# A graph network on one core: the edge matrix counted by 64 destinations and two source halves, and one-hots made eight tiles at a time

## The chip, the cores and the metric

The kernel runs on one core of one Trainium2 chip. The metric is the device time of one execution in microseconds (us). The kernel before takes 3625.48 us, the median of 10 runs (3618.81 to 3635.07).

The core's engines run side by side, each with its own instruction stream: TensorE (PE, matmuls into PSUM banks, with its weight loads shown as PEld), VectorE (DVE), ScalarE (ACT), GpSimd (POOL) and SyncE (SP). On GpSimd stand the indirect DMAs that gather rows from device memory by an index; SyncE issues most of the other DMAs.

## The reference

6250 nodes of 128 features, 100,000 edges sorted by destination, 8 edge types. Two networks follow each other, each added to its input and normalised:

```python
def _rgcn_conv(x, src, dst, etype, bases_l, comp_l, root_l, bias_l):
    weight = jnp.einsum('rb,bio->rio', comp_l, bases_l)
    h = jnp.einsum('ni,rio->nro', x, weight)
    msg = h[src, etype]
    seg = dst * R + etype
    cnt = jax.ops.segment_sum(jnp.ones((msg.shape[0],), dtype=x.dtype), seg, num_segments=N * R)
    norm = 1.0 / jnp.maximum(cnt[seg], 1.0)
    agg = jax.ops.segment_sum(msg * norm[:, None], dst, num_segments=N)
    return agg + x @ root_l + bias_l
...
# first network: 3 such layers, batch norm and relu behind the first two
# second network:
    h = x @ W_in + b_in
    deg = jax.ops.segment_sum(jnp.ones(row.shape[0], dtype=h.dtype), row, num_segments=N)
    deg_inv_sqrt = jnp.where(deg > 0, jax.lax.rsqrt(jnp.maximum(deg, 1.0)) * jnp.where(deg > 0, 1.0, 0.0), 0.0)
    edge_weight = deg_inv_sqrt[row] * deg_inv_sqrt[col]
    acc = h
    cur = h
    for _ in range(NUM_LAYERS):            # 3
        msgs = cur[col] * edge_weight[:, None]
        cur = jax.ops.segment_sum(msgs, row, num_segments=N)
        acc = acc + cur
    final = acc / (NUM_LAYERS + 1)
    return final @ W_out + b_out
```

In the second network `row` is the source and `col` the destination of an edge.

## The kernel before

Everything that runs is in one function, `sorted_path`; a second path behind a flag (`general_path`) is for inputs of another kind and does not run here. Nodes lie in 49 blocks of 128 (`NBLK`), edges in 782 tiles of 128 (`NTS`).

**The gathers and sums.** Each of the three layers of the first network goes over the edge tiles. For tile t, `one_sum` (line 1470) issues one indirect DMA on POOL that fetches 128 rows of 128 floats (line 1472) into `gt`, lets VectorE make a weighted one-hot `o` (line 1476: the edge's column compared with a row of numbers, times the edge's weight `norm`; 56 columns wide in the first kind of sum, 48 in the second), and lets PE multiply the two into a PSUM bank (line 1478). `gt` comes from a pool of 32 buffers (`gp`), `o` from one of 16 (`op`), the PSUM banks `ps` from one of 2, each holding 8 sums. Tiles 92 to 191 (`first_sums`, 100 gathers a layer) fetch rows of the layer's input x and VectorE adds the sum to `z` (line 1496). Tiles 192 to 781 (`window_sums`, 590 gathers a layer) fetch messages from `h_d`; two tiles share a sum, and VectorE adds it to `agg` (line 1526) at a column that a register holds. The messages of a layer, 49 blocks, are made during `first_sums` by `messages` (line 816: two matmuls of 512 columns on PE, copies on ScalarE, a DMA to `h_d`). Tiles 0 to 91 have no gathers: `dense_sums` (line 1180) does them with a small count matrix, in each layer after 400 tiles of the second kind; it loads that matrix in 7 pieces `packed1`.

**The side work.** `side_work` (line 1443) makes three things for later, in small steps that `take_turns` mixes with the tiles of all three layers, `N_SIDE` steps spread over `TURNS` tiles:
- `hot_counts` (line 1011) makes the count matrix for the first 92 tiles, written to `c1_d`.
- `degrees` (line 1257) counts edges per source: per four tiles VectorE makes `lo_hot` (line 1272, 4 x 128) and `blk_hot` (line 1275, 4 x 49), and PE multiplies them (line 1284).
- `counts` (line 1296) makes the whole edge matrix of the second network as small integers, seven counts in the bit fields of one int32 word (`NF` = 7, a field is 7 source blocks of 128, `S` = 896 columns). It works in 245 steps (`NST`) of 4 tiles. A step belongs to one block of 128 destinations. Per step VectorE makes `dst_hot` (line 1405, 4 x 128), and per tile a `row` (line 1409: `iota_c` compared with the edge's source column, times the value of its field, 896 wide); PE multiplies them in two halves of 448 columns (line 1420), two tiles behind (`LEAD` = 2); at a step's last tile VectorE adds the two PSUM banks to the running block `had` (line 1428, two instructions, times a flag that clears it at a new block), and SyncE writes the block to `a_d` (line 1437) under a condition that holds only where the block is done, at a place read from a register.

`rp` (4 buffers) holds `row`, `ac` (4) holds `had`, `cp` (2) holds `dst_hot`, `lo_hot` and `blk_hot`, `ps_w` (5 banks) every `pw`.

**The last stage.** Behind the layers the three rounds of the second network multiply the whole edge matrix with the nodes: per round and slice of sources, 7 loads of 448 KB from `a_d` (`packed`, line 1721), three masks on VectorE (lines 1725 and 1728) and 49 matmuls per load that read single bytes of the words as 8-bit floats (line 1736).

**What sets the order.** The kernel is written for the Tile framework: its scheduler fixes each engine's order when the kernel is built, and a tile's buffer is handed on when its last reader is done. Nothing is reordered at run time: an engine waits at each instruction for its semaphores. POOL's stream between the layers' starts is gathers alone.

## Time and profile before

| | |
|---|---|
| median of 10 runs | 3625.48 us (3618.81 to 3635.07) |
| the profiled execution | 3627.07 us, of which the span from first to last instruction 3625.3 us |
| PE (matmul) | 2835.5 us busy, 78% |
| PEld (weight load) | 2048.8 us, 57% |
| DVE | 2496.6 us, 69% |
| ACT | 320.5 us, 9% |
| POOL | 2169.1 us, 60% |
| mean granted PE clock | 0.734 of full speed |
| HBM | read 231.16 MB, written 211.53 MB |

The groups of instructions that the change touches (count, total busy time, mean of one):

| line | engine | what | count | busy us | mean ns |
|---|---|---|---|---|---|
| 1472 | POOL | gathers from `h_d` | 1770 | 1861.2 | 1052 |
| 1476 | DVE | `o`, 48 wide | 1770 | 476.9 | 324 |
| 1476 | DVE | `o`, 56 wide | 300 | 92.3 | 328 |
| 1478 | PE | sums of `gt` and `o` | 4140 | 968.9 | 348 |
| 1405 | DVE | `dst_hot` | 245 | 166.4 | 679 |
| 1409 | DVE | `row`, 896 wide | 980 | 491.5 | 513 |
| 1420 | PE | `row` x `dst_hot`, 448 columns | 1960 | 735.2 | 506 |
| 1428 | DVE | `had`, 448 columns | 490 | 311.1 | 673 |
| 1736 | PE | last stage, 193 columns | 7203 | 614.7 | 248 |

The share of an engine is an average over stages that have different limits: the layers run to about 2930 us of the span, and the last stage from there. "Busy" leaves out the issuing of DMAs and the handling of registers and semaphores. In lines of a timeline the columns are: start in us, duration in us, engine, line, operation, output and inputs, and in brackets the idle time of the engine before it with what ended it. In the table by stages (windows) each row gives from:to in us, the length, the busy time and number of instructions of each engine, the granted clock, the share of time that the DMA engines were busy and what they moved.

### The profile page before, as it was taken

What the parts mean: (1) busy time and instruction counts of PE and PEld (TensorE: products, weight loads), DVE (VectorE), ACT (ScalarE), POOL (GpSimd) and SP (SyncE); (2) the same over time, 40 slices, a digit from 0 to 9 for tenths busy, and PEclk for the clock granted to TensorE, in tenths of its full rate; (3) what the DMA queues carried; (4) which work ended last, traced back from release to release, by engine and by line L of the source; (5) the groups of instructions that cost most, each with busy time, mean ns of one, the idle gap of its engine ahead of it and who ended that gap; (6) DMA issues with size and microseconds to landing.
All of it is one profiled execution on the core that took longest, in us unless ns stands there. A gap on an engine that the chain in (4) does not pass through costs nothing.

```text
span 3625.3 us, 52477 instructions
## 1 busy us (share of the span) xinstructions
PE 2835.5 (78%) x16544; PEld 2048.8 (57%) x16544; DVE 2496.6 (69%) x7582; ACT 320.5 (9%) x586; POOL 2169.1 (60%) x2083
## 2 busy tenths in 40 slices
PE   5967555668769877877777797887777669999998
PEld 3545344445444455555545454554444469999997
DVE  8557797794782887777548559787764667566555
ACT  2500000001015100000100430000001020000000
POOL 5577897777747777777777477777777720000000
PEclk9955555578769855555776897556567779999998
DMA  5612201124138222222332762222223233333331
GB/s 175 239 52 66 71 21 48 50 56 101 51 87 307 81 61 60 61 66 65 96 76 66 244 221 76 70 71 72 76 80 87 66 102 109 114 112 114 108 117 32
DMA packets 255407, 347.15 MB, mean 96 GB/s; under 512 B 85926, under 2 KB 184078, under 8 KB 255124
## 3 DMA queue, kind: packets, MB, share of 16 engines
q1 hardware_dynamic: 180440, 204.30, 17.6%
q0 software_dynamic: 66240, 135.79, 14.5%
q10 hardware_dynamic: 8444, 3.61, 0.4%
q8 instruction: 138, 2.26, 0.3%
q14 instruction: 145, 1.19, 0.1%
HBM read 231.16 MB, written 211.53 MB: 122 GB/s over the span
## 4 chain that ended last, share of the span: by engine, by line
PE 45%; DMA 24%; DVE 18%; issue 9%; POOL 3%; DVEq 1%; ACT 0%; POOLq 0%; ACTq 0%; SPq 0%
DMA gt<-h_d,gidx 22%; PE pw L1736 16%; PE ps L1478 8%; PE pw L820 6%; PE pw L1420 6%; PE pw L1223 4%; DVE o L1476 3%; POOL gt L1472 3%; DVE row L1409 3%; DVE had L1428 2%; DVE lo_hot L1272 2%; DVE agg L1526 1%; PE pw L1250 1%; PE pw L833 1%; DVE dst_hot L1405 1%
## 5 line engine op out<-in xcount | busy, mean ns | idle before, releaser
L1472 POOL DMA_INDIRECT gt<-h_d,gidx x1770 | 1861.2, 1052 | 539.4 <-issue 198.7
L1478 PEld LDWEIGHTS ps<-o,gt 128*128 128x128 f32 x4140 | 907.0, 269 | 932.2 <-DVE o L1476 280.1
L1478 PE MATMUL ps<-o,gt 128*128 128x48 f32 (+1 forms) x4140 | 968.9, 348 | 545.4 <-DMA gt<-h_d,gidx 341.5
L1420 PE MATMUL pw<-row,dst_hot 128*128 128x448 bf16 x1960 | 735.2, 506 | 52.0 <-DVE row L1409 48.3
L1736 PE MATMUL pw<-three,u 128*128 128x193 bf16 x7203 | 614.7, 248 | 12.2 <-DVE three L1657 9.8
L1736 PEld LDWEIGHTS <-u 128*128 128x128 fp8e3 x7203 | 603.7, 98 | 18.0 <-issue 9.8
L1476 DVE TENSOR_SCALAR o<-iota_f,lo,norm 128x48 f32<-128x48 f32 x1770 | 476.9, 324 | 40.4 <-PE ps L1478 40.0
L1409 DVE TENSOR_SCALAR row<-iota_c,e_tab,e_tab 128x896 bf16<-128x896 int16 x980 | 491.5, 513 | 18.1 <-PE pw L1420 18.0
L1428 DVE SCALAR_TENSOR_TENSOR had<-had,keep,pw 128x448 int32<-128x448 int32 x490 | 311.1, 673 | 206.1 <-PE pw L1420 206.0
L1420 PEld LDWEIGHTS <-dst_hot 128*128 128x128 bf16 x1960 | 287.4, 162 | 218.3 <-issue 179.3
L820 PE MATMUL pw<-w,xT 128*128 128x512 f32 x588 | 289.3, 623 | 0.5 <-DVE xc L1584 0.3
L1472 POOL DMA_INDIRECT gt<-x_d,xidx x200 | 190.1, 951 | 134.3 <-DMA xc<-x_d 36.8
L1728 DVE TENSOR_SCALAR u<-packed 128x896 int32<-128x896 int32 x147 | 91.5, 622 | 187.4 <-PE pw L1736 185.1
L1476 DVE TENSOR_SCALAR o<-iota_f,hcol,norm 128x56 f32<-128x56 f32 x300 | 92.3, 328 | 156.8 <-PE ps L1478 156.3
L1526 DVE TENSOR_TENSOR agg<-agg,ps 128x48 f32 x885 | 171.9, 194 | 24.1 <-PE ps L1478 21.8
L821 ACT COPY hs<-pw 128x512 f32<-128x512 f32 x294 | 170.3, 586 | 172.2 <-PE pw L820 154.5
L1223 PE MATMUL pw<-x,u 128*128 128x385 bf16 x735 | 177.0, 380 | 0.0
L1725 DVE TENSOR_SCALAR u<-packed 128x896 int32<-128x896 int32 x294 | 174.5, 617 | 0.0
L1405 DVE TENSOR_TENSOR dst_hot<-iota_f,e_tab 128x512 bf16<-128x512 f32 x245 | 166.4, 679 | 0.0
L1272 DVE TENSOR_TENSOR lo_hot<-iota_f,e_tab 128x512 bf16<-128x512 f32 x196 | 133.1, 679 | 40.0 <-PE pd L1284 39.6
L820 PEld LDWEIGHTS pw<-w,xT 128*128 128x128 f32 x588 | 106.0, 197 | 87.9 <-issue 76.1
L1223 PEld LDWEIGHTS <-u 128*128 128x128 fp8e3 x882 | 100.8, 117 | 75.1 <-issue 37.5
(371 smaller groups left out, 1690.8 us busy)
## 6 DMA issues: line engine op xcount, KB each, us to landing
a_d<-had SPq DMA_DIRECT2D x245, 448.0 KB
h_d<-hs SPq DMA_DIRECT2D x147, 512.0 KB
packed<-a_d SPq DMA_DIRECT2D x147, 448.0 KB
gt<-h_d,gidx POOLq DMA_INDIRECT x1770, 2.6
c_d<-had SPq DMA_DIRECT2D x62, 196.0 KB
packed<-c_d SPq DMA_DIRECT2D x21, 448.0 KB
x_d<-xc SPq DMA_DIRECT2D x24, 256.0 KB
xc<-in_x_dram SPq DMA_DIRECT2D x19, 256.0 KB
```

Source lines behind the costliest of these rows:

```text
L820: nc.tensor.matmul(ph, xT[:, b * P : (b + 1) * P], w[:, c : c + 512], start=True, stop=True)
L1223: nc.tensor.matmul(sums[d][:, :C3D], us[d % 2][:, i, :, d // 2], x3[:, i, :], start=(c == 0 and i == 0), stop=(c * CH + i == NBLK - 1))
L1272: nc.vector.tensor_tensor(hot[:, :n, :], iota_f[:, None, :].to_broadcast([P, n, P]), src_lo[:, t0 : t0 + n, None].to_broadcast([P, n, P]), ...
L1405: nc.vector.tensor_tensor(hots[s], iota_f[:, None, :].to_broadcast([P, TS, P]), rel_s[:, s, :, None].to_broadcast([P, TS, P]), op=OP.is_equal)
L1409: nc.vector.tensor_scalar(rows[i], iota_c, e_src[:, s, j : j + 1], e_val[:, s, j : j + 1], op0=OP.is_equal, op1=OP.mult)
L1420: nc.tensor.matmul(p[:, :w], hots[s][:, j, :], row[:, c : c + w], start=(j == 0), stop=(j == TS - 1))
L1428: nc.vector.scalar_tensor_tensor(now[:, c : c + w], had[:, c : c + w], keep[:, s : s + 1], p[:, :w], op0=OP.mult, op1=OP.add)
L1472: nc.gpsimd.indirect_dma_start(out=gt, out_offset=None, in_=table, in_offset=bass.IndirectOffsetOnAxis(ap=at[:, t : t + 1], axis=0))
L1476: nc.vector.tensor_scalar(o[:, :width], iota_f[:, :width], column[:, t : t + 1], norm[:, t : t + 1], op0=OP.is_equal, op1=OP.mult)
L1478: nc.tensor.matmul(pa, gt, o[:, :width], start=first_, stop=last)
L1526: nc.vector.tensor_add(to, to, pa)
L1736: nc.tensor.matmul(out_of(f), bytes_[WHERE[f][0]][:, d, :, WHERE[f][1]], cur[:, order[c0 + d], :], start=(c0 + d == 0 and f == f0), stop=( ...
```

## The change

The edge matrix is counted by blocks of 64 destinations (`BD`, 98 blocks) and not 128. The 128 rows of a step's product are the 64 destinations, each once for the lower and once for the upper half of the 896 source columns: an edge whose source column is 448 or more gets its row number moved by 16384 (`FAR`), and `iota_h`, against which `dst_hot` compares, counts 0, 16384, 1, 16385 and so on. So `row` is 448 wide (`SH`), a tile takes one matmul and one PSUM bank, a step one add, and a block in `a_d` is one piece of 1792 bytes per partition. There are 294 steps in place of 245. `row` runs six tiles ahead of its matmul (`LEAD`), the add and the write come three steps of the loop behind the last matmul (`leave`, `LAG`).

The one-hots `o` of eight tiles are made by two instructions, one that compares and one that multiplies by the weights (`hot_columns`), half a batch ahead (`columns_of`).

Pools: `gp` 24 buffers in place of 32, `op` 3 tiles of eight one-hots in place of 16 of one, `rp` 10 (of half the width) in place of 4, `dst_hot` 3 in place of 2, `packed1` 2 in place of 1, loaded two pieces ahead. The last stage reads the same words from the new order of `a_d`, in 896 pieces of 512 bytes per load instead of 128 of 3584. The few instructions in `counts` that turned a block's number into its place (`fld`, `pos`) are gone.

```diff
--- before
+++ after
@@ -601,9 +601,15 @@
     TS = 4
+    BD = P // 2
+    NBD = NP // BD
+    SH = S // 2
+    FAR = 1 << 14
     NG4 = Q * J // TS
-    NST = NG4 + NBLK
-    LEAD = 2
+    NST = NG4 + NBD
+    LEAD = 6
+    LAG = 3
+    OB = 8
     CH = 7
...
@@ -680,8 +686,8 @@
     hp = tc.alloc_tile_pool(name="hp", bufs=3)
-    gp = tc.alloc_tile_pool(name="gp", bufs=32)
-    op = tc.alloc_tile_pool(name="op", bufs=16)
+    gp = tc.alloc_tile_pool(name="gp", bufs=24)
+    op = tc.alloc_tile_pool(name="op", bufs=3)
     xT = first.tile([P, NP], F32, name="xT")
...
@@ -981,15 +987,18 @@
     kp = tc.alloc_tile_pool(name="kp", bufs=1)
-    rp = tc.alloc_tile_pool(name="rp", bufs=4)
+    rp = tc.alloc_tile_pool(name="rp", bufs=10)
     ac = tc.alloc_tile_pool(name="ac", bufs=4)
     dn = tc.alloc_tile_pool(name="dn", bufs=1)
     cp = tc.alloc_tile_pool(name="cp", bufs=2)
 
 
-    a_d = dram.tile([NSL, P, NBLK, P], I32, name="a_d")
-    iota_c = kp.tile([P, S], mybir.dt.int16, name="iota_c")
-    nc.gpsimd.iota(iota_c, pattern=[[1, S]], base=0, channel_multiplier=0)
+    a_d = dram.tile([NBD, P, SH], I32, name="a_d")
+    iota_c = kp.tile([P, SH], mybir.dt.int16, name="iota_c")
+    nc.gpsimd.iota(iota_c, pattern=[[1, SH]], base=0, channel_multiplier=0)
+    iota_h = kp.tile([P, P], F32, name="iota_h")
+    nc.gpsimd.iota(iota_h.rearrange("p (d q) -> p d q", q=2), pattern=[[1, BD], [FAR, 2]], base=0,
+                   channel_multiplier=0, allow_small_or_imprecise_dtypes=True)
     iota_s = kp.tile([P, NST], F32, name="iota_s")
...
@@ -1184,16 +1194,16 @@
         def load(c):
-            packed = dn.tile([P, SUB, CH, R], I32, name="packed1")
+            packed = dn.tile([P, SUB, CH, R], I32, name="packed1", bufs=2)
             nc.sync.dma_start(packed, c1_d[:, :, c * CH * R : (c + 1) * CH * R]
                               .rearrange("p s (d r) -> p s d r", r=R))
             return packed, [(k, n, rows_of(x_d[l], c * CH + k, n, nc.sync)) for k, n in ((0, 4), (4, CH - 4))]
 
-        ready = load(0)
+        ready = [load(0), load(1)]
         for _ in range(3):
             yield
         for c in range(NBLK // CH):
-            packed, parts = ready
+            packed, parts = ready.pop(0)
             nc.scalar.copy(x3[:, :4, :D], parts[0][2])
...
@@ -1215,8 +1225,8 @@
                                         x3[:, k : k + n, D : 2 * D], op=OP.subtract)
-            if c + 1 < NBLK // CH:
-                ready = load(c + 1)
+            if c + 2 < NBLK // CH:
+                ready.append(load(c + 2))
             yield
...
@@ -1390,54 +1388,55 @@
         nc.vector.scalar_tensor_tensor(e_src, e_fld, -float(S), e_src, op0=OP.mult, op1=OP.add)
+        upper = over
+        nc.vector.tensor_scalar(upper, e_src, float(SH), None, op0=OP.is_ge)
+        nc.vector.scalar_tensor_tensor(e_src, upper, -float(SH), e_src, op0=OP.mult, op1=OP.add)
+        nc.vector.scalar_tensor_tensor(rel_s, upper, float(FAR), rel_s, op0=OP.mult, op1=OP.add)
         yield
 
-        pieces = [(c, S // 2) for c in range(0, S, S // 2)]
-        had = ac.tile([P, S], I32, name="had")
+        had = ac.tile([P, SH], I32, name="had")
         nc.vector.memset(had, 0)
-        at = {}
+        at, runs = {}, [had]
         rows, hots, sums = {}, {}, {}
-        for i in range(NST * TS + LEAD):
-            s, j = divmod(i, TS)
-            if s < NST:
-                if j == 0:
-                    hots[s] = cp.tile([P, TS, P], BF16, name="dst_hot")
-                    nc.vector.tensor_tensor(hots[s], iota_f[:, None, :].to_broadcast([P, TS, P]),
-                                            rel_s[:, s, :, None].to_broadcast([P, TS, P]),
-                                            op=OP.is_equal)
-                rows[i] = rp.tile([P, S], BF16, name="row")
-                nc.vector.tensor_scalar(rows[i], iota_c, e_src[:, s, j : j + 1], e_val[:, s, j : j + 1],
-                                        op0=OP.is_equal, op1=OP.mult)
-            if i < LEAD:
-                yield
-                continue
-            s, j = divmod(i - LEAD, TS)
-            open_sums[0] = j < TS - 1
-            if j == 0:
-                sums[s] = [ps_w.tile([P, 512], F32, name="pw") for _ in pieces]
-            pa, row = sums[s], rows.pop(i - LEAD)
-            for (c, w), p in zip(pieces, pa):
-                nc.tensor.matmul(p[:, :w], hots[s][:, j, :], row[:, c : c + w], start=(j == 0),
-                                 stop=(j == TS - 1))
-            if j < TS - 1:
-                yield
-                continue
-            del sums[s], hots[s]
-            now = ac.tile([P, S], I32, name="had")
-            for (c, w), p in zip(pieces, pa):
-                nc.vector.scalar_tensor_tensor(now[:, c : c + w], had[:, c : c + w], keep[:, s : s + 1],
-                                               p[:, :w], op0=OP.mult, op1=OP.add)
+
+        def leave(s):
+            now = ac.tile([P, SH], I32, name="had")
+            nc.vector.scalar_tensor_tensor(now, runs.pop(), keep[:, s : s + 1], sums.pop(s)[:, :SH],
+                                           op0=OP.mult, op1=OP.add)
             if s % REGS == 0:
-                for k, top_ in ((0, NBLK - 1), (1, 1)):
+                for k, top_ in ((0, NBD - 1), (1, 1)):
                     _, v = nc.values_load_multi_w_load_instructions(
                         step_i[0:1, k, s : min(s + REGS, NST)], engines=[ET.SP], min_val=0, max_val=top_,
                         skip_runtime_bounds_check_because=IN_RANGE)
                     for i, x_ in enumerate(v):
                         at[k, s + i] = x_
-            nc.sync.dma_start(
-                a_d[:, :, bass.ds(at[0, s], 1), :].rearrange("s p d c -> p s (d c)"),
-                now.rearrange("p (s c) -> p s c", c=P), cond=(at[1, s] == 1))
-            had = now
+            nc.sync.dma_start(a_d[bass.ds(at[0, s], 1), :, :].rearrange("b p c -> p b c"),
+                              now[:, None, :], cond=(at[1, s] == 1))
+            runs.append(now)
+
+        for i in range(NST * TS + LEAD + LAG):
+            s, j = divmod(i, TS)
+            if s < NST:
+                if j == 0:
+                    hots[s] = cp.tile([P, TS, P], BF16, name="dst_hot", bufs=3)
+                    nc.vector.tensor_tensor(hots[s], iota_h[:, None, :].to_broadcast([P, TS, P]),
+                                            rel_s[:, s, :, None].to_broadcast([P, TS, P]),
+                                            op=OP.is_equal)
+                rows[i] = rp.tile([P, SH], BF16, name="row")
+                nc.vector.tensor_scalar(rows[i], iota_c, e_src[:, s, j : j + 1], e_val[:, s, j : j + 1],
+                                        op0=OP.is_equal, op1=OP.mult)
+            s, j = divmod(i - LEAD, TS)
+            if 0 <= s < NST:
+                open_sums[0] = j < TS - 1
+                if j == 0:
+                    sums[s] = ps_w.tile([P, 512], F32, name="pw")
+                nc.tensor.matmul(sums[s][:, :SH], hots[s][:, j, :], rows.pop(i - LEAD), start=(j == 0),
+                                 stop=(j == TS - 1))
+                if j == TS - 1:
+                    del hots[s]
+                    ending.append(lambda s=s: leave(s))
+            if ending and (i - LEAD - LAG) % TS == TS - 1:
+                ending.pop(0)()
             yield
...
@@ -1467,15 +1466,39 @@
 
-    def one_sum(pa, table, at, column, width, t, first_, last):
+    def hot_columns(column, width, t0, n):
+        o = op.tile([P, OB, HC], F32, name="o")
+        nc.vector.tensor_tensor(o[:, :n, :width], iota_f[:, None, :width].to_broadcast([P, n, width]),
+                                column[:, t0 : t0 + n, None].to_broadcast([P, n, width]), op=OP.is_equal)
+        nc.vector.tensor_tensor(o[:, :n, :width], o[:, :n, :width],
+                                norm[:, t0 : t0 + n, None].to_broadcast([P, n, width]), op=OP.mult)
+        return o
+
+    def columns_of(column, width, t_first, t_end):
+
+        made = {}
+
+        def make(b):
+            t0 = t_first + b * OB
+            if t0 < t_end:
+                made[b] = hot_columns(column, width, t0, min(OB, t_end - t0))
+
+        def of(t):
+            b, k = divmod(t - t_first, OB)
+            if t == t_first:
+                make(0)
+            if k == OB // 2:
+                made.pop(b - 1, None)
+                make(b + 1)
+            return made[b][:, k, :width]
+        return of
+
+    def one_sum(pa, table, at, columns, t, first_, last):
         gt = gp.tile([P, D], F32, name="gt")
         nc.gpsimd.indirect_dma_start(
             out=gt, out_offset=None, in_=table,
             in_offset=bass.IndirectOffsetOnAxis(ap=at[:, t : t + 1], axis=0))
-        o = op.tile([P, HC], F32, name="o")
-        nc.vector.tensor_scalar(o[:, :width], iota_f[:, :width], column[:, t : t + 1],
-                                norm[:, t : t + 1], op0=OP.is_equal, op1=OP.mult)
-        nc.tensor.matmul(pa, gt, o[:, :width], start=first_, stop=last)
+        nc.tensor.matmul(pa, gt, columns(t), start=first_, stop=last)
 
...
@@ -1501,7 +1525,7 @@
             pa = bank[:, k % GPB, :]
-            one_sum(pa, x_d[l], xidx, hcol, HC, t, True, True)
+            one_sum(pa, x_d[l], xidx, columns, t, True, True)
             waiting.append((t, pa))
...
@@ -1540,6 +1565,8 @@
                     side_until(side_done[0] + 1)
+                while ending:
+                    ending.pop(0)()
                 assert counted[0] and degrees_known[0]
...
@@ -1718,7 +1745,9 @@
                 packed = ap_.tile([P, CH, P], I32, name="packed")
-                nc.sync.dma_start(packed, a_d[sl, :, c0 : c0 + CH, :])
+                nc.sync.dma_start(packed, bass.AP(
+                    tensor=a_d.tensor, offset=a_d.offset + c0 // CH * P * S + sl * P,
+                    ap=[[S, P], [NSL * P * S, CH], [1, P]]))
                 u = up.tile([P, len(PICK), CH, P], I32, name="u")
...
```

## The prediction

> **What bounds the kernel now.** I read the busy table first (PE 78%, VectorE 69%, POOL 60%): no engine stands out as an average, so I cut the span by stages and counted POOL's instructions in each.
>
> ```profile
> core 0: us, PE busy (x) PEld busy (x) DVE busy (x) ACT busy (x) POOL busy (x), PEclk, DMA share, GB/s
> 114.00:428.00 314.00, 233.99 (x880) 156.42 (x878) 195.36 (x777) 39.45 (x65) 237.44 (x249) 0.62 0.34 104
> 428.00:500.00 72.00, 26.78 (x316) 23.31 (x315) 72.00 (x165) 0.00 (x0) 69.56 (x9) 0.50 0.10 26
> 500.00:700.00 200.00, 115.44 (x784) 98.20 (x785) 155.54 (x500) 0.24 (x1) 156.73 (x143) 0.50 0.18 47
> 700.00:1050.00 350.00, 258.33 (x1148) 165.74 (x1147) 251.95 (x751) 14.68 (x26) 270.67 (x260) 0.72 0.26 67
> 1230.00:1988.00 758.00, 595.68 (x2311) 380.58 (x2310) 565.12 (x1672) 14.68 (x26) 582.48 (x577) 0.63 0.26 69
> 2230.00:2925.00 695.00, 522.09 (x2052) 337.78 (x2050) 475.42 (x1447) 14.16 (x25) 532.91 (x531) 0.64 0.28 74
> 3000.00:3626.00 626.00, 608.95 (x6993) 591.95 (x6990) 378.24 (x1061) 30.66 (x84) 0.00 (x0) 0.98 0.34 101
> ```
>
> In these rows POOL runs only gathers. One takes 0.94 us and the next starts 0.30 us later whatever the releaser named, so the floor is 1.248 us each (timeline, next fence). 249 gathers need 310.8 of the first row's 314 us, although PE and VectorE differ widely between rows. So from 114 to 2925 us POOL's row of gathers is the path, and a row's loss is its length less gathers times 1.248: 3, 61, 21.5, 25.5, 38 and 32 us. Between layers POOL idles 37 and 35 us more. After 3000 us PE is the bound, at clock 0.98.
>
> Where do the losses come from? From gathers that last longer than 0.94 us:
>
> ```profile
> 1526.10 0.97 POOL L1472 DMA_INDIRECT gt<-h_d,gidx  x1 [0.30 <-DMA gt<-h_d,gidx]
> 1527.26 0.68 DVE L1405 TENSOR_TENSOR dst_hot<-iota_f,e_tab 128x512 bf16<-128x512 f32 x1
> 1527.38 1.38 POOL L1472 DMA_INDIRECT gt<-h_d,gidx  x1 [0.31 <-issue]
> 1529.06 0.94 POOL L1472 DMA_INDIRECT gt<-h_d,gidx  x1 [0.30 <-issue]
> ```
>
> VectorE's one-hot began 0.12 us before the gather and ended 0.56 us into it; the gather lasted 0.44 us too long. Going through such pairs gives one rule: a gather needs something of VectorE's some 0.125 us after its start; if a TENSOR_TENSOR on two SBUF tiles, or a wide `row`, began at least 0.06 us before the gather, the gather waits until it ends. Back to back such instructions starve POOL altogether:
>
> ```profile
> 441.83 0.34 DVE L1275 TENSOR_TENSOR blk_hot<-iota_f,e_tab 128x196 bf16<-128x196 f32 x1
> 441.89 57.15 POOL L1472 DMA_INDIRECT gt<-h_d,gidx  x1 [0.30 <-issue]
> 442.10 0.68 DVE L1272 TENSOR_TENSOR lo_hot<-iota_f,e_tab 128x512 bf16<-128x512 f32 x1
> ```
>
> That one gather lasted 57 us, under a burst of some 65 `blk_hot`/`lo_hot` pairs.
>
> **What the change relieves.** VectorE: two rows of 896 back to back start 0.42 us apart, two of 392 (line 1153) 0.29, so 448 gives 0.305: 980 x 0.42 = 412 becomes 1176 x 0.305 = 359. The adds start 0.60 apart: 490 become 294, 118 us less. `dst_hot`, 0.60 each, 245 become 294: 29 more. The narrow one-hots `o` start 0.215 apart, 2070 of them, 445 us; they become 259 pairs of TENSOR_TENSOR over 384 or 448 elements, some 0.47 us each (0.60 for 512, less 128 of 1 ns), 250 us. In all some 340 us off VectorE. PE: 784 of 1960 matmuls of 735 us go, 294 us. I cost all this at nothing: both engines follow the gathers (PE starts a sum some 1.6 us after its gather's end in most stretches), VectorE was busy 565 of 758 us, and less work does not start a gather sooner. It would count only if POOL's floor went away. SyncE's 49 more conditional writes (73 ns each to issue), the registers for them, the constants on POOL and the second dense buffer lie under the same cover. The last stage reads `a_d` in 896 pieces of 512 B per load, not 128 of 3584 B. In the packet records the 3584 B pieces take 0.19 us each and the 512 B pieces of the writes 0.027 to 0.033, so the same total; one write of 896 pieces passes in 1.6 to 1.75 us, a load now in 2.0, and the last stage needs one each 4.2 us with ten buffers. Cost 0; were they twice as slow they would still fit.
>
> **What it adds on the path.**
>
> (A) 24 gather buffers for 32, at the start.
>
> ```profile
> 67.50 1.31 POOL L1472 DMA_INDIRECT gt<-in_x_dram,xidx  x1 [0.30 <-issue]
> 104.44 0.88 POOL L992 IOTA iota_c<- 128x896 int16 x1 [35.63 <-PE pw L765]
> 114.97 0.96 POOL L1472 DMA_INDIRECT gt<-in_x_dram,xidx  x1 [9.28 <-PE ps L1478]
> ```
>
> POOL fills 32 buffers, then waits for PE's first sum. With 24 it has 8 gathers fewer behind it there: 8 x 1.25 = 10 us. In the built order 13 message blocks stand ahead of that first sum instead of 9; 18 matmuls of theirs took 10.4 us, so 4 blocks (8 matmuls) are 4.6 us. Sum 14; bounds 8 and 17.
>
> (B) The same buffers at the start of layer 3, where messages fill PE and it falls behind:
>
> ```profile
> 2143.06 0.94 POOL L1472 DMA_INDIRECT gt<-x_d,xidx  x1 [0.77 <-PE ps L1478]
> 2145.04 1.00 POOL L1472 DMA_INDIRECT gt<-x_d,xidx  x1 [1.03 <-PE ps L1478]
> ```
>
> POOL already touches the limit: 40 us of gathers in flight. 24 buffers hold 30, so 10 us; layer 2 peaks at 31.5, so 2. Sum 12; bounds 0 (PE catches up by its lighter load) and 15.
>
> (C) More instructions that hold gathers up. The new `o` is two TENSOR_TENSORs on SBUF tiles, the form of `dst_hot`; the old one held a gather for next to nothing (0.30 us long). The price of an unbroken stretch of C us, hit at random by gathers 1.25 apart, is (C - 0.185)^2 / 2.5. In the trace a gather gets in ahead of a `row` (46 of 46 after `dst_hot`, 42 of 47 after another row), but not between a `row` and the `dst_hot` behind it (1 of 17). So I cut VectorE's built order ahead of each row. Before, past the degrees: 931 lone rows (0.50 us) x 0.039 + 196 lone `dst_hot` (0.68) x 0.096 + 49 row-`dst_hot` (1.10) x 0.33 = 71 us; the table has 25.5 + 38 + 32 = 96. After: 902 rows (0.39) 14 us, 229 lone `o` (0.55) 12, 134 `dst_hot` 13, 124 row-`dst_hot` (0.98) 31, 115 row-`o` (0.85) 20, 18 row-`o`-`dst_hot` (1.46) 11, 17 with a second `o` (1.93) 19, some ten longer 8: 128. That is +57, or +77 with the ratio 96 to 71. I take 70. Bounds: if every instruction stood alone, rows, `dst_hot` and `o` give 74 us against 62 before, +12; if no gather got in anywhere inside a stretch, 284 against 147, +137.
>
> (D) The degrees (500 to 700 us). Old `o`, 0.43 us for two, let gathers in between `blk_hot` and `lo_hot`; the new ones don't, and PE's order puts eight sums in a row and then up to ten and more groups of degrees. The same price gives 19 us before if a gather gets in ahead of `blk_hot`, 40 if not (measured 21.5), and 34 or 77 after: +15 to +56 (the ratio 21.5 to 19 makes it +17). I take 25, as the clumps lengthen the stretches. The 57 us burst keeps its length (130 instructions, now 132): 0.
>
> Sum: 14 + 12 + 70 + 25 = +121 us on the profiled span 3625.3, whose execution took 3627.1; the median is 3625.5, so some 3746.
>
> **A rule that speaks against (C).** The Trainium skill, "SBUF — State Buffer", section "Who interferes with whom", has tensor_tensor take only the read side of the port pair that VectorE shares with GpSimd, infers that descriptor generation needs the write side, and so lets tensor_scalar stall such DMAs but not tensor_tensor. By it the new `o` would be free, (C) would only have its rows become cheaper (36 us to 14), (D) nothing, and the sum would be 3627 + 26 - 22 = 3631. The rows above differ: `dst_hot` is a tensor_tensor and its gather waited to its end.
>
> **The rivals.**
> - Less VectorE work leaves POOL alone: stretches break up and fall between gathers, as at 114 to 428 us, where 249 gathers lost 3 us. At 0.013 us each the 1368 gathers of the last three gather rows lose 18, not 96: -78 + 26 = -52, 3573. For it: VectorE idles more. Against: the built order has longer unbroken stretches, and PE's clumps release rows in bursts. It decides if the three rows lose under 70 us. Chance 0.16.
> - Only the buffers count, (C) +12 and (D) 0: 3627 + 38, 3663. For it: waits inside the stretches, which let a gather in where the built order alone shows none. Chance 0.17.
> - Nothing moves, PE's lighter load buying back the buffers: 3625. Chance 0.05.
> - Every stretch at full price: 26 + 137 + 50 = +213, 3838. For it: the 57 us burst, which obeyed the full price. Chance 0.13.
>
> **How the numbers follow.** My forecast has 0.49: 3746, by its own terms 3690 to 3800 on the slow side, which stands beside the range since a case of the other sign has weight. The range 3615 to 3850 takes in the rivals but the first (0.16) and the upper part of the last. About 0.2% (7 us) is what a measurement can tell from no change: faster 0.16, same 0.05, slower 0.79 (0.49 + 0.17 + 0.13).
>
> **What would show it.** (A) The second batch of gathers starts near 119 us with 24 behind it, not 32. (B) POOL idles some 10 us on PE's sums near 2150. (C) Gathers past the degrees average over 1.05 us, not near 1.01; their rows of the table lose 150 to 180 us. (D) The 140 gathers behind the burst lose 35 to 50. PE and VectorE are less busy by some 300 us each, and the last stage keeps its 600 us. I am wrong if the gathers keep their mean, or if the last stage waits on `packed`.

## The result, and the profile after

The changed kernel takes 3686.41 us (median of 8 runs, 3681.68 to 3697.79) against 3625.35 us (28 runs of before, measured with it): a ratio of 1.0172, 95% interval 1.0161 to 1.0183, so 61 us slower. Its profiled execution has a span of 3684.0 us. The table by stages of the changed kernel, with the cuts of before (busy time and number of instructions per engine, granted clock, DMA share, GB/s):

```profile
428.00:500.00 72.00, 27.91 (x326) 24.21 (x325) 72.00 (x167) 0.00 (x0) 69.56 (x9) 0.50 0.13 33
700.00:1050.00 350.00, 245.72 (x1007) 157.08 (x1007) 202.67 (x554) 13.66 (x24) 265.43 (x259) 0.66 0.26 66
1230.00:1988.00 758.00, 515.51 (x1919) 334.89 (x1918) 428.08 (x1209) 13.52 (x24) 582.52 (x565) 0.62 0.25 66
2230.00:2925.00 695.00, 480.27 (x1774) 313.14 (x1774) 386.60 (x1070) 14.17 (x25) 536.17 (x522) 0.60 0.27 74
```

VectorE is busy 428 us of 758, where it was 565; POOL got through 565 gathers in that time, where it did 577. The row loses 758 - 565 x 1.248 = 53 us (38 before), the one of layer 3 43.5 (32), the one of layer 1 27 (25.5). PE's relief went into waiting. Its sums and counting matmuls in the groups, first two lines before, last two after (busy, mean ns | idle before):

```profile
L1478 PE MATMUL ps<-o,gt 128*128 128x48 f32 (+1 forms) x4140 | 968.9, 348 | 545.4 <-DMA gt<-h_d,gidx 341.5
L1420 PE MATMUL pw<-row,dst_hot 128*128 128x448 bf16 x1960 | 735.2, 506 | 52.0 <-DVE row L1409 48.3
L1501 PE MATMUL ps<-o,gt 128*128 128x48 f32 (+1 forms) x4140 | 994.6, 370 | 649.8 <-DMA gt<-h_d,gidx 600.1
L1433 PE MATMUL pw<-row,dst_hot 128*128 128x448 bf16 x1176 | 467.2, 545 | 22.6 <-DVE row L1426 22.2
```

The counting matmuls fell from 735 to 467 us, and the waits of the sums for gathers grew from 341.5 to 600.1. The timeline of POOL in the changed kernel, at the start and in layer 3:

```profile
53.09 1.66 POOL L1498 DMA_INDIRECT gt<-in_x_dram,xidx  x1 [0.30 <-issue]
104.17 0.51 POOL L998 IOTA iota_c<- 128x448 int16 x1 [49.42 <-PE pw L771]
117.03 0.96 POOL L1498 DMA_INDIRECT gt<-in_x_dram,xidx  x1 [11.14 <-PE ps L1501]
...
2160.03 1.33 POOL L1498 DMA_INDIRECT gt<-x_d,xidx  x1 [1.00 <-PE ps L1501]
2161.97 0.94 POOL L1498 DMA_INDIRECT gt<-x_d,xidx  x1 [0.61 <-PE ps L1501]
2163.91 0.94 POOL L1498 DMA_INDIRECT gt<-x_d,xidx  x1 [1.00 <-PE ps L1501]
```

The 24th gather starts at 53.09 us and the 25th at 117.03; from 2157 to 2191 most gathers wait for a sum. At the end of the dense part (here layer 2) POOL also waits, which it did not before:

```profile
1929.38 3.06 PE L1260 MATMUL pw<-z,w 128*128 128x400 f32 x4
1932.26 2.45 PE L1433 MATMUL pw<-row,dst_hot 128*128 128x448 bf16 x12
1936.33 0.91 PE L1501 MATMUL ps<-o,gt 128*128 128x48 f32 x7
1936.95 1.28 POOL L1498 DMA_INDIRECT gt<-h_d,gidx  x1 [3.64 <-PE ps L1501]
```

The next thing to see is a gather under the new one-hots (timeline of all engines, changed kernel):

```profile
1505.28 0.39 DVE L1426 TENSOR_SCALAR row<-iota_c,e_tab,e_tab 128x448 bf16<-128x448 int16 x1
1505.59 0.55 DVE L1473 TENSOR_TENSOR o<-o,norm 128x384 f32<-128x384 f32 x1
1505.75 1.80 POOL L1498 DMA_INDIRECT gt<-h_d,gidx  x1 [0.30 <-PE ps L1501]
1506.05 0.68 DVE L1422 TENSOR_TENSOR dst_hot<-iota_h,e_tab 128x512 bf16<-128x512 f32 x1
1506.65 0.39 DVE L1426 TENSOR_SCALAR row<-iota_c,e_tab,e_tab 128x448 bf16<-128x448 int16 x1
```

`o` began 0.16 us ahead of the gather, `dst_hot` followed without a pause, and the gather lasted 0.86 us too long: it waited through both, to 1506.73 (1505.75 + 0.125 + 0.86), where `dst_hot` ended. It got in ahead of the `row`.

From the start and end of each of the 2070 gathers I added up, for every run, what lies on POOL's path (us). "Held" is the gathers' time over 0.944 us each; gathers 32 to 290 hold the burst of degrees before and after, 291 to 433 the rest of the degrees, 434 to 2069 all that is past them. "Other pauses" are gaps over 0.304 us past gather 32, without the two between layers. Each row is one execution, and its time can lie up to 10 us from the median of its kernel's runs (e1, e3 and e6 are 8 to 9 us under it, e5 6 and e8 9 us over it).

| run | start of gather 32 | held 32-290 | held 291-433 | held past | other pauses | last gather to end | span |
|---|---|---|---|---|---|---|---|
| before | 115.0 | 66.4 | 21.3 | 104.0 | 3.4 | 700.6 | 3625.3 |
| after | 127.1 | 73.2 | 28.5 | 122.8 | 23.5 | 694.2 | 3684.0 |
| e1_gt32 | 116.1 | 77.3 | 28.7 | 112.8 | 2.3 | 700.2 | 3653.3 |
| e2_old_o | 122.6 | 89.9 | 24.4 | 82.3 | 22.6 | 698.0 | 3654.4 |
| e3_gt32_old_o | 113.2 | 88.8 | 22.4 | 73.0 | 5.5 | 703.2 | 3620.4 |
| e4_before_new_o | 116.8 | 67.1 | 20.3 | 143.0 | 2.6 | 702.3 | 3679.4 |
| e5_lo_ts | 112.7 | 4.0 | 7.8 | 96.9 | 41.0 | 713.2 | 3590.7 |
| e6_all_ts | 113.6 | 3.6 | 16.5 | 17.5 | 62.6 | 700.5 | 3528.7 |
| e7_ob4 | 128.9 | 5.9 | 138.4 | 82.1 | 30.7 | 699.7 | 3699.3 |
| e8_dst_ts | 128.5 | 73.2 | 29.6 | 52.8 | 23.4 | 701.0 | 3624.0 |

After less before: 12.1 at the start, 6.8 + 7.2 + 18.8 held, 20.1 of pauses, -6.4 at the end; with 0.1 between the layers that is the span's 58.7 us. The -6.4 is no gain that repeats: e1, e2, e3, e7 and e8 have the same last stage and took 698.0 to 703.2 us from the last gather to the end.

### The profile page after: what moved, and what is told of

Same layout as the page of the kernel before. It is cut to its first block, busy times and chain, and to the rows that moved or that the text cites. A ratio compares the mean times of both kernels' runs of the same rounds, so it can differ in the third digit from the quotient of the medians.

```text
span 3684.0 us, 47720 instructions
## 1 busy us (share of the span) xinstructions
PE 2707.7 (73%) x15760; PEld 1992.0 (54%) x15760; DVE 2159.9 (59%) x6076; ACT 320.8 (9%) x586; POOL 2197.8 (60%) x2084
## 4 chain that ended last, share of the span: by engine, by line
PE 42%; DMA 27%; DVE 11%; issue 7%; POOL 4%; DVEq 0%; ACT 0%; POOLq 0%; SPq 0%; ACTq 0%
DMA gt<-h_d,gidx 26%; PE pw L1765 16%; PE ps L1501 8%; PE pw L1433 6%; PE pw L826 5%; POOL gt L1498 4%; PE pw L1233 3%; DVE lo_hot L1282 3%; PE pw L1260 1%; DVE row L1426 1%; PE pw L1172 1%; DVE agg L1551 1%; DVE row L1163 1%; DVE had L1177 1%; PE pw L839 1%
## 5 line engine op out<-in xcount | busy, mean ns | idle before, releaser
L1501 PE MATMUL ps<-o,gt 128*128 128x48 f32 (+1 forms) x4140 | 994.6, 370 | 649.8 <-DMA gt<-h_d,gidx 600.1
L1501 PEld LDWEIGHTS ps<-o,gt 128*128 128x128 f32 x4140 | 877.2, 279 | 934.5 <-DMA gt<-h_d,gidx 764.4
L1426 DVE TENSOR_SCALAR row<-iota_c,e_tab,e_tab 128x448 bf16<-128x448 int16 x1176 | 451.6, 397 | 352.4 <-PE pw L1433 352.3
L1765 PEld LDWEIGHTS <-u 128*128 128x128 fp8e3 x7203 | 603.8, 98 | 18.0 <-issue 9.8
L1433 PE MATMUL pw<-row,dst_hot 128*128 128x448 bf16 x1176 | 467.2, 545 | 22.6 <-DVE row L1426 22.2
L1422 DVE TENSOR_TENSOR dst_hot<-iota_h,e_tab 128x512 bf16<-128x512 f32 x294 | 201.6, 686 | 162.0 <-PE pw L1433 161.2
L1433 PEld LDWEIGHTS <-dst_hot 128*128 128x128 bf16 x1176 | 187.6, 168 | 182.3 <-issue 144.3
L1404 DVE SCALAR_TENSOR_TENSOR had<-had,keep,pw 128x448 int32<-128x448 int32 x294 | 197.3, 671 | 15.0 <-PE pw L1433 15.0
L1471 DVE TENSOR_TENSOR o<-iota_f,lo 128x384 f32<-128x384 f32 x222 | 121.6, 548 | 124.4 <-PE ps L1501 124.3
L1473 DVE TENSOR_TENSOR o<-o,norm 128x384 f32<-128x384 f32 (+2 forms) x261 | 146.0, 561 | 0.2
L1498 POOL DMA_INDIRECT gt<-in_x_dram,xidx x100 | 113.0, 1130 | 48.6 <-PE ps L1501 16.6
```

Of the source, the lines that this page charges most:

```text
L1404: nc.vector.scalar_tensor_tensor(now, runs.pop(), keep[:, s : s + 1], sums.pop(s)[:, :SH], op0=OP.mult, op1=OP.add)
L1422: nc.vector.tensor_tensor(hots[s], iota_h[:, None, :].to_broadcast([P, TS, P]), rel_s[:, s, :, None].to_broadcast([P, TS, P]), op=OP.is_equal)
L1426: nc.vector.tensor_scalar(rows[i], iota_c, e_src[:, s, j : j + 1], e_val[:, s, j : j + 1], op0=OP.is_equal, op1=OP.mult)
L1433: nc.tensor.matmul(sums[s][:, :SH], hots[s][:, j, :], rows.pop(i - LEAD), start=(j == 0), stop=(j == TS - 1))
L1498: nc.gpsimd.indirect_dma_start(out=gt, out_offset=None, in_=table, in_offset=bass.IndirectOffsetOnAxis(ap=at[:, t : t + 1], axis=0))
L1501: nc.tensor.matmul(pa, gt, columns(t), start=first_, stop=last)
```

## The experiments

**Which part of the change costs what.** Four runs undo or take alone the buffers and the one-hots `o`: e1 has 32 gather buffers again (room for them from two small pools), e2 makes `o` tile by tile again with 16 buffers, e3 does both (with 10 row buffers), and e4 puts the change's `hot_columns` and `columns_of` alone into before.

```diff
--- after
+++ e1_gt32
-    gp = tc.alloc_tile_pool(name="gp", bufs=24)
+    gp = tc.alloc_tile_pool(name="gp", bufs=32)
...
-    rp = tc.alloc_tile_pool(name="rp", bufs=10)
+    rp = tc.alloc_tile_pool(name="rp", bufs=9)
...
-            packed = dn.tile([P, SUB, CH, R], I32, name="packed1", bufs=2)
+            packed = dn.tile([P, SUB, CH, R], I32, name="packed1")
...
--- after
+++ e2_old_o
-    op = tc.alloc_tile_pool(name="op", bufs=3)
+    op = tc.alloc_tile_pool(name="op", bufs=16)
...
-        nc.tensor.matmul(pa, gt, columns(t), start=first_, stop=last)
+        o = op.tile([P, HC], F32, name="o")
+        nc.vector.tensor_scalar(o[:, :width], iota_f[:, :width], column[:, t : t + 1],
+                                norm[:, t : t + 1], op0=OP.is_equal, op1=OP.mult)
+        nc.tensor.matmul(pa, gt, o[:, :width], start=first_, stop=last)
...
```

> After with 32 gather buffers (room for them: packed1 single and loaded one piece ahead, row buffers 9). Theory: the 24 buffers cost some 33 us of the 61 (POOL's waits for PE's sums grew by 36 us, 16 of them at the start, the first gathers were held 4 us less), and the gathers held by VectorE the rest. So the pause of the first layer falls from 62 to about 50 us, the waits near 973, 1212, 1933 and 2157 to 2191 us go, and the time is 3650 to 3658. Rival: PE's order (matmuls six tiles behind, clumps ahead of the sums) makes the waits and more buffers only put them off; then the time stays over 3672.

> After with the one-hots o made tile by tile with one instruction each, as before (16 buffers), all else as after. Theory: the two wide instructions per eight tiles hold gathers up, so the gathers' time over 0.944 us each, 240 us in all in after, falls by 15 to 30 us and the time is 3655 to 3672. Rival: the batches relieve VectorE and rows and dst_hot are what holds; then it stays at 3686 or is slower.

> After with both undone: 32 gather buffers (packed1 single) and o tile by tile. What is left of the change is the edge matrix by 64 destinations and two halves with its order. Theory: the two effects add, and what is left is a gain of some 5 us in the last stage and a few in the gathers: 3615 to 3635. Rival: the wide steps themselves (294 dst_hot for 245, steps run further ahead) hold gathers: over 3645.

> Before with only the one-hots o made eight tiles at a time by two instructions. Theory: gathers are held 15 to 30 us more in all, 3640 to 3657. Rival: 195 us less of VectorE's work let gathers through sooner, 3625 or less; or, if stretches of row, dst_hot (896 columns wide here) and o run on unbroken, as the prediction had it: over 3680.

Measured, as a ratio to before in the same set (3632.0 us): e1 1.0089 (1.0076 to 1.0102), e2 1.0068 (1.0055 to 1.0081), e3 0.9999 (0.999 to 1.0007), e4 1.0126 (1.0111 to 1.014). Against after's 1.0172 the buffers are worth 30 us (0.0083 x 3632), `o` 38 us, both together 63. The effects add within some 5 us, and the whole loss is these two parts. The median of e1, 3663, lies between its two expectations and misses both, but its pauses are gone (23.5 to 2.3), so the rival (PE's order makes them) falls. e2 and e3 came as their theories had it. e4 missed: `o` alone costs 46 us, not 15 to 30. Held past the degrees it has 39 us more than before, the same as after against e2 (40.5) and e1 against e3 (39.8); of the 54 us between the two profiled spans, 12.7 more lie between the layers, which I had not expected and did not follow up.

That e3 equals before doesn't mean that the new edge matrix, with its order, does nothing. It holds gathers 31 us less past the degrees (73.0 for 104.0), and gives 22 back in the burst: there one gather lasted 73 us for 57. In the built order 162 instructions of the degrees stand in a row in e3, 130 in before, 132 in after.

**Is it the form of the instruction?** The burst's `lo_hot` (e5, on before) and `dst_hot` (e8, on after, against `iota_h` as int16, one piece ahead of each row) are made from narrow instructions with a scalar operand per partition, which takes VectorE longer. e6 has both edits on e3. e7 is after with batches of four and 6 buffers for them.

```diff
--- before
+++ e5_lo_ts
-                nc.vector.tensor_tensor(hot[:, :n, :], iota_f[:, None, :].to_broadcast([P, n, P]),
-                                        src_lo[:, t0 : t0 + n, None].to_broadcast([P, n, P]),
-                                        op=OP.is_equal)
+                for j in range(n):
+                    nc.vector.tensor_scalar(hot[:, j, :], iota_b, src_lo[:, t0 + j : t0 + j + 1], None,
+                                            op0=OP.is_equal)
--- after
+++ e8_dst_ts
-    iota_h = kp.tile([P, P], F32, name="iota_h")
+    iota_h = kp.tile([P, P], mybir.dt.int16, name="iota_h")
...
-                    nc.vector.tensor_tensor(hots[s], iota_h[:, None, :].to_broadcast([P, TS, P]),
-                                            rel_s[:, s, :, None].to_broadcast([P, TS, P]),
-                                            op=OP.is_equal)
+                hot = hots[s]
+                nc.vector.tensor_scalar(hot[:, j, :], iota_h, rel_s[:, s, j : j + 1], None, op0=OP.is_equal)
--- after
+++ e7_ob4
-    OB = 8
+    OB = 4
...
-    op = tc.alloc_tile_pool(name="op", bufs=3)
+    op = tc.alloc_tile_pool(name="op", bufs=6)
```

> Before with lo_hot (the degrees' one-hots) made by four tensor_scalars of 128 columns against a bf16 row, each with its column as a scalar operand, in place of one tensor_tensor of 512. VectorE works longer by that, not less. Theory: a gather gets in ahead of an instruction that has a scalar operand read per partition, so the one gather of 57 us goes; POOL runs on until its 32 buffers are full (40 us) and then waits some 25 to 35 us for PE. Gain 25 to 40 us with the degrees behind the burst: 3585 to 3605. Rival: what counts is how long VectorE works on SBUF tiles without a pause, whatever the form: the long gather stays, 60 us or more, and the time is 3625 to 3645.

> After with 32 gather buffers (packed1 single), o tile by tile, and lo_hot and dst_hot by four tensor_scalars each (dst_hot against an int16 row). Theory: the burst of degrees costs 40 to 50 us in place of 79, the gathers past it are held 30 to 40 us in place of 72, the degrees in between 10 in place of 22: 3545 to 3575. Rival (form does not matter, VectorE's time does): 3630 to 3660.

> After with the one-hots o made four tiles at a time (6 buffers of half the size): twice as many instructions of half the width. Theory: the price grows with the square of a stretch's length, so shorter pieces hold gathers less and some 10 to 20 us of the 35 that the batches of eight cost come back: 3665 to 3676. Rival: each such instruction holds what it holds, or longer stretches are made of more pieces: 3683 or slower.

> After with dst_hot alone made by four tensor_scalars (int16 row, column as scalar operand), one ahead of each row. Theory: dst_hot, 0.69 us long and often behind a row, is the dearest piece left, and o behind a row comes next: gain 20 to 35 us, 3650 to 3666. Rival: the form does not matter and VectorE's time grows: 3686 or slower.

Before took 3626.89 us in this set. e5: 3586.21, ratio 0.9884 (0.9869 to 0.9899). e6: 3538.71, 0.9765 (0.975 to 0.9779). e7: 3699.88, 1.0204 (1.019 to 1.0218). e8: 3616.33, 0.9969 (0.9957 to 0.9982). The timeline of e5, inside the burst and at its end:

```profile
441.23 0.35 DVE L1275 TENSOR_TENSOR blk_hot<-iota_f,e_tab 128x196 bf16<-128x196 f32 x1
441.39 1.00 POOL L1472 DMA_INDIRECT gt<-h_d,gidx  x1 [0.30 <-DMA gt<-h_d,gidx]
441.50 0.91 DVE L1273 TENSOR_SCALAR lo_hot<-iota_b,e_tab 128x128 bf16<-128x128 bf16 x4
442.15 0.35 DVE L1275 TENSOR_TENSOR blk_hot<-iota_f,e_tab 128x196 bf16<-128x196 f32 x1
442.69 1.01 POOL L1472 DMA_INDIRECT gt<-h_d,gidx  x1 [0.30 <-issue]
...
463.39 1.16 POOL L1472 DMA_INDIRECT gt<-h_d,gidx  x1 [0.30 <-PE pd L1284]
500.94 3.42 POOL L1472 DMA_INDIRECT gt<-h_d,gidx  x1 [36.39 <-PE ps L1478]
```

VectorE is as full as it was, and the gathers pass at 1.0 us each: the 57 us gather is gone. What comes next is close to what was expected: with its buffers full POOL waits 36.4 us for the first sum behind the burst. e8 gained twice what its theory had (3650 to 3666): in it VectorE works on `dst_hot` for 322 us where after has 202, and the kernel is 70 us faster; the gathers past the degrees are held 52.8 us for 122.8, as much as the whole gain. e6 came 6 us under its range: the gathers past the degrees are held 17.5 us, less than expected, and the burst costs 3.6 us and a pause of 55, more than expected. The timeline of e6 at a place like the one shown of after:

```profile
1501.27 0.51 DVE L1474 TENSOR_SCALAR o<-iota_f,lo,norm 128x48 f32<-128x48 f32 x2
1501.45 0.94 POOL L1470 DMA_INDIRECT gt<-h_d,gidx  x1 [0.30 <-PE pw L1432]
1501.70 0.24 DVE L1423 TENSOR_SCALAR dst_hot<-iota_h,e_tab 128x128 bf16<-128x128 int16 x1
1501.87 0.63 DVE L1425 TENSOR_SCALAR row<-iota_c,e_tab,e_tab 128x448 bf16<-128x448 int16 x1
1502.70 0.94 POOL L1470 DMA_INDIRECT gt<-h_d,gidx  x1 [0.30 <-DMA gt<-h_d,gidx]
```

Four kinds of instruction back to back, and both gathers take 0.94 us. So the rival, that VectorE's time alone counts, falls in all three runs: its busy time in all rose by 7 us in e5 (over before), 33 in e8 (over after) and 43 in e6 (over e3), and each became faster. e6 beats before by 2.35% and after by 4%.

That it is the form alone is not shown. The edits also make each instruction narrower, 128 columns for 512, and change the type of the row that it compares with; four narrow tensor_tensors were not run. For the form speaks that gathers got in ahead of a `row`, a tensor_scalar 896 wide, but hardly ever ahead of a `dst_hot` (the prediction's counts on before). Against it alone speaks e7, where `o` is still made by tensor_tensors, half as wide: of the gathers that came under a `dst_hot` with the second instruction of `o` right behind it, 19 of 20 got in between the two, in after 2 of 13.

To see what holds, I put each delay past the degrees down to the VectorE instruction that ended where the delay did (within 0.08 us; us in all; the rest lies with the dense part or with no single instruction):

| | `dst_hot` | `o` | `row` |
|---|---|---|---|
| before | 34 | 14 | 24 |
| after | 65 | 40 | 10 |
| e2_old_o | 56 | 0.3 | 9 |
| e3_gt32_old_o | 49 | 0.2 | 11 |
| e7_ob4 | 40 | 24 | 11 |
| e8_dst_ts | 0.2 | 29 | 11 |
| e6_all_ts | 0.3 | 0.5 | 8 |

e7 splits. Past the degrees the gathers are held 82.1 us for 122.8, as little as with `o` tile by tile (82.3), which looks like the theory. But by the table only 16 of these 41 us are of `o` (24 for 40); 25 are of `dst_hot` (40 for 65), whose form and width e7 leaves alone. So length is shown to count for 16 us at most; the other 25 may lie with the built order, which changed too. And the time is 12 us longer than after's, as the rival had it. The scheduler put the burst together anew, 254 instructions of the degrees in a row for 132, and one gather among them lasted 115.5 us:

```profile
515.92 115.46 POOL L1498 DMA_INDIRECT gt<-h_d,gidx  x1 [0.30 <-issue]
```

**Can the burst be spread, and what is the matrix worth without it?** e9 makes `blk_hot` of e6 in the buffers of `o`. e10 and e12 are one kernel, before with the edits of e5 and e8; e11 is after with the same two.

```diff
--- e6_all_ts
+++ e9_paced
-                blk = cp.tile([P, TS, NBLK], BF16, name="blk_hot")
+                blk = [op.tile([P, HC], F32, name="o").bitcast(BF16)[:, :NBLK] for _ in range(n)]
                 for j in range(n):
+                    nc.vector.tensor_scalar(blk[j], iota_b[:, :NBLK], src_blk[:, t0 + j : t0 + j + 1], None,
+                                            op0=OP.is_equal)
...
-                nc.vector.tensor_tensor(blk[:, :n, :],
...
```

> The fastest so far (after with 32 gather buffers, o tile by tile, lo_hot and dst_hot by tensor_scalars), with blk_hot also made tile by tile, in the ring of 16 buffers that o uses: a group of the degrees can then be built at most 16 such buffers ahead of the sums, so that it can't stand in one burst ahead of them. Theory: the remaining pause of 55 us, in which POOL with its buffers full waits for PE's sums behind the burst, goes, at most 10 us come back as shorter waits: 3485 to 3505. Rival: the degrees' work takes VectorE's and PE's time wherever it stands and the pause only spreads: 3525 to 3545.

> Before with lo_hot and dst_hot by four tensor_scalars each; rows of 896, one matmul per half, the order as before. Beside the run with the same edit on the new edge matrix it shows what that matrix is worth once hardly any gather is held. Theory: the path is POOL's row of gathers, and VectorE's and PE's relief counts only through held gathers, of which the rows of 896 still hold some 25 to 40 us against 17; but the burst here is shorter (57 against 79 us): 3535 to 3560, within 20 us of the other. Rival: the relief of PE and VectorE is worth its time: over 3575.

> After, with lo_hot and dst_hot by four tensor_scalars each, and its 24 buffers and batches of o kept. Theory: past the degrees the gathers stay held by some 50 us (o alone or behind a row), the long gather of 58 us goes and POOL then waits 40 to 50 us for PE, as 24 buffers hold 30 us of gathers: 3585 to 3605. Rival: in the burst the batches of o, or what remains of the tensor_tensors (blk_hot), still starve a gather for 20 us or more: over 3610.

> The kernel of e10 once more, since in that set even before took 4109 us, 13% more than ever, with 150 waits of POOL that the profile puts down to something outside the core. Theory as there: the path is POOL's row of gathers, so what the new edge matrix takes off PE (300 us) and VectorE is worth next to nothing once gathers are not held: 3535 to 3560, within 20 us of the same edit on the new matrix (3538.7). Rival: the relief of PE and VectorE is worth time of its own: over 3575.

None of these times can be set beside the others or beside what was expected of them, since in these two sets before itself took 4108.78 and 4131.29 us. Against before in the same set: e9 0.9948 (0.9928 to 0.9968), e10 0.9989 (0.9977 to 1.0001), e11 1.0114 (1.0091 to 1.0137), e12 0.999 (0.9978 to 1.0001). The waits of VectorE in e12 (waited for: us in total, times, longest):

```profile
DVE had L1427 <- remote: 200.1, 59, 9.4
DVE row L1408 <- remote: 96.3, 28, 7.0
DVE z L1495 <- remote: 68.9, 6, 31.9
DVE row L1153 <- remote: 67.4, 11, 13.6
```

VectorE stands still for 3 us and more at a time for something outside the core's own records, and POOL itself does so 156 times, 209 us in all. PE runs some 40 us behind the gathers past the degrees, so all 32 buffers are full, and POOL waits 401 us for sums, where it was 121 in before's profile. I read it so that the path is no longer POOL's row of gathers, and that a gather held then costs next to nothing: the two edits, of which the first alone gained 1.2% on before and the second 2.0% on after, gain 0.1% together, which can't be told from nothing. What the pauses come from was not tried, and what the edge matrix is worth with no gather held stays open. e9 does show one thing of its own, in its timeline (first two lines; the third is the pause of e10, of the same set):

```profile
390.94 0.94 POOL L1468 DMA_INDIRECT gt<-h_d,gidx  x1 [1.86 <-PE pw L1172]
458.05 0.94 POOL L1468 DMA_INDIRECT gt<-h_d,gidx  x1 [66.17 <-PE ps L1474]
609.64 0.95 POOL L1471 DMA_INDIRECT gt<-h_d,gidx  x1 [74.18 <-PE ps L1477]
```

The degrees no longer stand in one burst (at most 16 of their VectorE instructions in a row, 406 in e6), but a pause is still there, 66 us where e10, with a burst, has 74, and it comes earlier: now the matmuls of `hot_counts` (line 1172) stand ahead of the sums. The theory that the pause goes with the burst fell; pacing one piece of side work let another run ahead here.

## Why the prediction was right or wrong

The direction and the path held, and 3686 lies in the range. The size did not: +121 was expected on the span and +59 came, just under the 3690 that the forecast's own terms allowed. Of the 59, 32 us are buffers (12.1 at the start, 20.1 of pauses), where (A) and (B) had 26; 33 are held gathers (6.8, 7.2 and 18.8), where (C) and (D) had 95; the rest is the -6.4 at the end. So 3686 lies nearer to the rival "only the buffers count" (3663) than to 3746, and some of its height is luck: 9.3 us of the pauses stand in no term, and the burst's 6.8 had been put at 0. The prediction's own signs say the same. The gathers past the degrees were to average over 1.05 us and came to 1.019, from 1.008; their rows were to lose 150 to 180 us and lost 123; the gathers behind the burst were to lose 35 to 50 and lost 28.5.

- *The relief costs nothing and gains nothing by itself.* Right. VectorE is 337 us less busy; PE's counting matmuls take 268 us less (its total fell by 128 only, which I did not trace further). PE's relief ended in waits for gathers. The exception is what the prediction called a rival: by e3 the matrix with its order saved 31 us past the degrees.
- *(A) the start, 14.* Right: 12.1, with 24 gathers ahead of the pause as foretold; the second batch began at 117.0 for 119, and e1 takes it back.
- *(B) the buffers later, 12.* 2.4 us in layer 2 and 8.4 in layer 3, as predicted (2 and 10). Missed: 9.3 us more near 973 and 1933, at the end of the dense part, where PE runs several clumps of `z` and counting matmuls ahead of the sums; 40 us of buffers covered that and 30 do not.
- *(C) held past the degrees, 70.* The step that failed. The cut of VectorE's order priced after at 128 us, and 122.8 came; it priced before at 71, and there are 104 by the gathers' sum (96 by the table's rows). So the difference was +18.8. Of the 51 us that 70 is too high, 33 are before priced too low, 13 what I added for the missing part of before, which I took as a factor (96 to 71) and laid on after too, and 5 after priced too high. The table by instruction shows what was missing: in before `dst_hot`, `o` and `row` hold 72 of 104 us, in after 115 of 122.8, so what lies with anything else is 32 us before and 8 after. It did not grow with the stretches, it shrank (13 in e3, which has the new matrix and the old `o`); why, no run shows. And the old `o`, priced at next to nothing, has 14 us in before. The parts are larger than their sum: the new `o` costs 39 to 41 us (e4, e2), the matrix gains 31 (e3).
- *(D) the degrees, 25.* Mis-sized: 7.2, under the lower bound of 15. The burst's 0 was 6.8 with what lies before it, and it goes with the built order: the longest gather took 57, 58, 73 and 115.5 us in before, after, e3 and e7, under 130, 132, 162 and 254 instructions of the degrees in a row.
- *The last stage, 0.* Right: it took 6.4 us less, and the runs with the same last stage lie from 694 to 703, so no difference is shown.
- *Rivals.* "Less VectorE work leaves POOL alone" was half true, of the matrix; "only the buffers count" (3663) falls as a cause with e1, which has the buffers back and stays 0.89% slower, though its sum came nearer than mine; the full price fell with (C).

The inference that the prediction weighed, in the Trainium skill's "SBUF — State Buffer", section "Who interferes with whom", that tensor_tensor does not stall such DMAs because it leaves the write side of the shared ports alone, does not carry over to these gathers. In the prediction's rows a gather waited to the end of a `dst_hot`, and e8 and e5, which put tensor_scalars in the place of one tensor_tensor each, gained 2.0% and 1.2% with more VectorE work. The same section has a two-input instruction contend with GpSimd's reads of SBUF, which the prediction did not weigh: these gathers read their indices from a tile in SBUF (`gidx`). Whether it is this read that waits, no run here shows.

## What to carry to other kernels

Where GpSimd's indirect DMAs set the pace, as here, a VectorE instruction is priced by the gathers that it holds, not by its own length: one `dst_hot` 512 wide cost more than four narrow ones with a scalar operand that together take longer (e8). Look for what needs buffers before giving them up for the relief of an engine that is not the path; here 24 for 32 cost 30 us. Where an estimate misses the measured row of before, find out which instructions hold the missing part before carrying it over to after; here it was 32 us, and 8 were left. And after each edit look again at what the scheduler put together: a change of batch size turned a burst of 132 instructions into one of 254 (e7).

## What was not expected

- One change of form and width, `dst_hot` by four tensor_scalars, was worth 2.0%, more than the whole change cost, though `dst_hot` itself then takes VectorE 120 us longer (VectorE's busy time in all rose by 33).
- Two sets in which before itself ran 13 and 14% longer, with VectorE standing still 59 times for 3.4 us ahead of `had` alone (e12): two edits that pay elsewhere bought 0.1% there.
- Batches of four went with as little holding past the degrees as single one-hots (82.1 and 82.3 us), batches of eight with 41 us more, but most of that lay on `dst_hot` and not on `o`.
